# Layers 2 and 3 of a four-layer mixture kernel: activations of a bank's halves behind both halves' passes, and TensorE's order by a written plan of 359 steps

## The chip, the cores and the metric

One Trainium2 chip, one core of it. The metric is the device time of one launch in microseconds (us), the median of several runs. The core has TensorE (PE), VectorE (DVE), ScalarE (ACT), GpSimd (POOL) and SyncE (SP), each with its own instruction queue, worked off in order, and DMA engines that the queues hand transfers to. [...]

## The reference

The input x has 4 rows of 512 tokens with 256 features. Four layers follow one another, each of the form `x = x + ffn(cond(x))`. They are counted from 1 here. This case is about layers 2, 3 and the first row of layer 4:

```python
# layer 2: cond is one matrix per row; ffn is 15 experts, the best 3 of each token, and a shared expert
z   = x @ w_bot[b].T + bias
top_p, top_i = top_k(softmax(z @ router_W + router_b), 3)
routed = sum over the 3:  top_p * (relu(z @ eW1[e] + eb1[e]) @ eW2[e] + eb2[e])
x   = x + relu(z @ sW1 + sb1) @ sW2 + sb2 + routed
# layer 3: cond is W_base plus a low-rank part mixed by the row's cond; ffn is for half of the tokens
z   = x @ (W_base + 2 * sum_e w[e] Bs[e] As[e]).T + b_base
top_s, top_i = top_k(z @ w_router, 256)
up  = sigmoid(top_s) * (gelu(z[top_i] @ W1 + b1) @ W2 + b2)
x   = x + scatter_add(z, top_i, up)
# layer 4, cond: a shared gated MLP and the row's 2 best of 8 gated MLPs (hidden size 1024 each)
z   = mlp(x; shared) + sum over 2:  w * mlp(x; skill)      # mlp: (gelu(x Wg) * (x Wu)) Wd
```

All matrices are float32.

## The kernel before, in words

x of row b is kept transposed in SBUF, `x[b]` of 128 partitions by 2 by 512 tokens. A matmul's group of passes goes to one PSUM bank (`bank()`); most matmuls of all layers are recorded by one helper, `mm`, and so stand at line L102 of the profile, told apart by their tiles.

The kernel is written as Python generators: every part of the work yields between steps, and helpers interleave them. `weave(main, side, r)` takes r steps of `side` after each of `main`; `zipped` takes one of each in turn; `late(items, begin, end, lag)` begins an item and ends the one `lag` before it. Inside `tc.manual_schedule(engines={...})` the engines named keep the order in which the code issues; everywhere else a planner of the framework orders each engine's instructions by its own costs. The first layer is already written so: `in_turn(parts, FIRST_PLAN)` takes the generators' next steps in the order of a string, for TensorE alone. From layer 2 on, `other_layers()` (L1909 on) weaves the parts loosely, and the planner orders all engines until near the kernel's end.

The parts that matter, with the letters that the plan gives them:

- **E**, `l1_experts` (L1193): tokens are grouped by expert in 62 units of 128 tokens, worked in 38 blocks (24 pairs, 14 single units); the first 54 units hold all that row 0 needs. Each block has four stages: `fetched` (its expert's 512 KB of weights by SP; one indirect gather per unit by POOL, L1212, from the rows in `zd` into a tile `hs`), `turned` (transposes on TensorE, L1226, a copy on DVE, L1228), `hidden` (four matmuls into the two halves of one bank, and an ACT Relu with bias for each half, L1240, into a tile `bc` of which there are three), and `down` (matmuls that the profile writes as bank<-w,bc, a DVE copy, L1252, and a write to HBM, `yd<-bc`, L1253). The stages of a block lie 0, 2, 3 and 4 blocks behind.
- **Q**, `l1_places`, and **W**, `l2_weights`: small; index arithmetic on DVE, and layer 3's matrix per row.
- **S2, S3**, `l1_shared` of rows 2 and 3 (rows 0 and 1 were done before): the shared expert.
- **K0 to K3**, `l1_combine`: 12 indirect gathers per row from `yd` (POOL, L1302: 4 tiles of tokens, 3 experts each), scaled on ACT (L1311) and added on DVE (L1313), then 8 transposes (L1319) and an add to x (L1320).
- **D0 to D3**, `l2_cond`: matmuls x,p into z (ACT, L1367), the router's score (z,wr; ACT, L1374), z's rows written to HBM, a rank of the 512 scores on DVE (L1380 to L1418, ending in a tile `at`), a matmul s_token,at, then `who` on DVE, `x += z` on POOL (L1441), and two gathers of the chosen rows (POOL, L1444).
- **F0 to F3**, `l2_ffn`: transposes (L1457), four pairs of hidden passes with an ACT Gelu for each half of the bank (L1471), down passes, a bias add (DVE, L1484), the write `yd2` to HBM (L1486).
- **G0 to G3**, `l2_back`: four gathers (POOL, L1493), scaled on ACT (L1500), transposed (L1502), added to x (DVE, L1504).
- **X**, `l3_cond(0)`: row 0 of layer 4, 24 steps of four x,w and two a,w matmuls of 128x512 with a Gelu (L1545) and a product (L1551), its weights loaded by SP (`in_w3c`, 512 KB each).

Row 0 goes first: K0, D0, F0, G0 and X depend on each other in this order, and rows 1 to 3 follow beside. After X come `l3_prepare` (its first matmuls are bank<-w,pe) and rows 1 to 3 of layer 4 with the attention woven in.

In `hidden` of both E and F the code was, for each half of the bank, the passes and then its activation. The next half's passes go to the same bank, which the activation reads, and the framework makes them wait for it.

Of the kernel before, what the change touches and what calls it, by code (L numbers as in the profile page):

```python
# [21 lines left out]
KD = D // P  # L22
NT = S // P
FIRST_PLAN = """C0*3 L C0*10 H0 C1*2 H0*3 P C1*2 H0*3 C1*2 P H0 P C1*2 P H0 C1 L H0*2 P C1 H0 C1 H0*3 C1*2 P H0 H1 P C2 H1*4 P*2 C2*2 P H1*2 C2*2 H1 P*2 H1 P C2 H0 H1 P C2 H0 H1 C2 P C2 H1 H0 H1 C2 P H1*2 C2 P H1*2 C2*2 P*2 H1 T0*3 P T0 L H2 P*2 C3 H2*3 C3 H1 H2 P C3*3 P*2 H2 P H2 U0 C3*3 H2*2 P*2 H2 P*2 H2 C3 H2*2 P H2 C3 U0 H2 P*2 C3 H2*2 C3*2 H3*2 P U0 P U0*2 P H2 H3*2 U0*4 H3 U0 H3 U0*2 H3 U0 H3 U0*3 H2 H3 U0*4 H3*2 U0*4 H3 U0 J0 H3 U0 B U0*2 H3 U0 H3 U0*10 B*2 U0*3 B U0 H3 U0*3 H3*2 T1*3 U0 U1 U0 U1*3 T1 P U1 U0 U1*7 J0*3 U1*3 J0 U1*2 J0 U1*4 J0 A0 H3 U1 A0 U1*2 J0 U1 A0*3 U1 A0 U1*3 A0 U1 A0 J1 A0 U1*3 J1 U1*2 J1*3 U1 A0 J1*2 U1*2 A1 U1*2 A1 U1 A1*2 J2 U1*4 A1*2 U1*2 A1 U1 J2*2 L A1 O0 A1 O0 J2 U1 O0 A1 O0*7 J1 J2 O0 J2*2 O1 O0*3 J2 O0 A2 O0 O1 O0 A2 O1*3 R0 A2 R0 O1*2 A2 O1 A2*2 O1*4 J3 A2 O0 J3 O1 R0 A2 O1 J3 O1 A2 R0 J3 R0*2 J3 R0*6 J3 R0 A2 J3 O1*2 R0 O1 R0 A3 R0*4 J3 A3*2 R1*2 R0*2 A3 R1 R0 A3 R1*4 A3 R1 A3*2 R1*3 O2 R0 O2*2 R1*2 A3 R1 O2*2 A3 R1*2 O2 R1 O2*7 R1*2 O3 O2 R1*2 O3 O2*2 R1*2 O3 O2 O3*2 R2 O3*3 R2*2 O3 R2*3 O3 R2*2 O3 R2*5 R0 R2 O3*2 R1 O2 R2*2 O3*3 R2 O3 R3*2 R2*2 R3*2 O3 R3*2 R2 S0 R3 R2 R3 S0*3 R3 R2*2 R3*5 S1 R3*2 R2 S1 R3*7 V R3 V*3 S1*2"""

NEG = -1e30

# [26 lines left out]
def kernel(  # L54
# [1138 lines left out]
    def l1_experts():  # L1193

        pairs = [((g + 1) / EARLY, 2 * g, 2) for g in range(EARLY)]
        alone = [((i + 0.5) / SINGLES, 2 * EARLY + i, 1) for i in range(SINGLES)]
        blocks = [b[1:] for b in sorted(pairs + alone)] + [(j, 2) for j in range(FIRST, LIVE, 2)]
        rows = yd.rearrange("(u p) f -> u p f", p=P)
        held = {}

        def owner(j):
            return nc.values_load(
                table["of"][0:1, j : j + 1], engines=[mybir.EngineType.SP], min_val=0, max_val=14,
                skip_runtime_bounds_check_because="from the table, which holds no others",
            )

        def fetched(s):
            j, n = blocks[s]
            w = weight(ws[W_EXP + owner(j)])
            t = new(apool, [P, KD, S], "hs", bufs=4)  # L1210
            for u in range(n):
                nc.gpsimd.indirect_dma_start(  # L1212
                    out=t[:, 0, u * D : (u + 1) * D],
                    out_offset=None,
                    in_=zd[:, :],
                    in_offset=bass.IndirectOffsetOnAxis(ap=table["who"][:, j + u : j + u + 1], axis=0),
                )
            held[s] = w.rearrange("p (l k f) -> p l k f", l=2, k=KD), t

        def turned(s):  # L1220
            j, n = blocks[s]
            t = held[s][1]
            pt = bank().rearrange("p (k t) -> p k t", k=KD)
            for u in range(n):
                for k in range(KD):
                    nc.tensor.transpose(pt[:, k, tok(u)], t[:, 0, u * D + k * P :][:, :P], ident)  # L1226
            xT = t[:, 1].rearrange("p (k t) -> p k t", k=KD)
            nc.vector.tensor_copy(xT[:, :, : n * P], pt[:, :, : n * P])  # L1228

        def hidden(s):  # L1230
            j, n = blocks[s]
            w, t = held[s]
            xT = t[:, 1].rearrange("p (k t) -> p k t", k=KD)
            hy = new(apool, [P, 2, S], "bc", bufs=3)
            h = hy[:, 0].rearrange("p (m t) -> p m t", m=KD)
            ph = bank().rearrange("p (m t) -> p m t", m=KD)
            for m in range(KD):
                for k in range(KD):
                    mm(ph[:, m, : n * P], w[:, 0, k, tok(m)], xT[:, k, : n * P], k == 0, k == KD - 1)
                nc.scalar.activation(  # L1240
                    h[:, m, : n * P], ph[:, m, : n * P], AF.Relu, bias=table["bias"][:, m, j : j + 1]
                )
            held[s] = w, hy, h

        def down(s):
            j, n = blocks[s]
            w, hy, h = held.pop(s)
            py = bank()
            for u in range(n):
                for k in range(KD):  # L1250
                    mm(py[:, u * D : (u + 1) * D], h[:, k, tok(u)], w[:, 1, k], k == 0, k == KD - 1)
            nc.vector.tensor_copy(hy[:, 1, : n * D], py[:, : n * D])  # L1252
            nc.sync.dma_start(  # L1253
                out=rows[j : j + n].rearrange("u p f -> p u f"),
                in_=hy[:, 1, : n * D].rearrange("p (u f) -> p u f", f=D),
            )

        for s in range(len(blocks) + 4):
            for stage, lag in ((fetched, 0), (turned, 2), (hidden, 3), (down, 4)):
                if 0 <= s - lag < len(blocks):  # L1260
                    stage(s - lag)
            yield

    rows1 = {}

# [30 lines left out]
    def l1_combine(b):  # L1296
        got = []
        for r in range(3):
            got.append(new(wpool, [P, 1024], "w").rearrange("p (i f) -> p i f", i=NT))
        for i in range(NT):  # L1300
            for r in range(3):
                nc.gpsimd.indirect_dma_start(  # L1302
                    out=got[r][:, i],
                    out_offset=None,
                    in_=yd[: FIRST * P] if b == 0 else yd[:, :],
                    in_offset=bass.IndirectOffsetOnAxis(ap=rows1[b][:, r, i : i + 1], axis=0),
                )
        yield
        for i in range(NT):
            y = got[0][:, i]  # L1310
            nc.scalar.activation(y, y, AF.Copy, scale=gate1[b][:, 0, i : i + 1])  # L1311
            for r in range(1, 3):
                nc.vector.scalar_tensor_tensor(y, got[r][:, i], gate1[b][:, r, i : i + 1], y, ALU.mult, ALU.add)  # L1313
            if i % 2:
                yield
        for k in range(KD):
            pk = bank()
            for i in range(NT):
                nc.tensor.transpose(pk[:, tok(i)], got[0][:, i, tok(k)], ident)  # L1319
            nc.vector.tensor_add(x[b][:, k], x[b][:, k], pk)  # L1320
        yield


    z2, gate2, who2, back2, y2 = {}, {}, {}, {}, {}
# [36 lines left out]
    def l2_cond(b):  # L1361
        z = new(apool, [P, KD, S], "z", bufs=3)
        for m in range(KD):
# [1 line left out]
            for k in range(KD):  # L1365
                mm(pz, w2m[b // 2][:, b % 2, k, tok(m)], x[b][:, k], k == 0, k == KD - 1)
            nc.scalar.activation(z[:, m], pz, AF.Identity, bias=col("b_base", m))  # L1367
        yield

        psc = bank()  # L1370
        for k in range(KD):
            mm(psc, wr[:, k], z[:, k], k == 0, k == KD - 1)
        sc = new(apool, [P, S], "t", bufs=4)
        nc.scalar.copy(sc, psc)  # L1374
        zd2 = new(dram, [S, D], "zd2", bufs=2)
        run(rows_to_dram(z, zd2))
        sown = small([P, NT], "sown")
        unused = new(apool, [P, S], "pe", BF16)
        for i in range(NT):
# [71 lines left out]
    def l2_ffn(b):  # L1451
# [11 lines left out]
        def hidden(f2):  # L1463
            ph = bank().rearrange("p (f t) -> p f t", f=2)
            h = new(apool, [P, 2, D], "p4", bufs=4)
            for j in range(2):
                f = 2 * f2 + j
                wa = w2a[f // 4].rearrange("p (k f) -> p k f", k=KD)
                for k in range(KD):
                    mm(ph[:, j], wa[:, k, tok(f % 4)], xT[:, k], k == 0, k == KD - 1)  # L1470
                nc.scalar.activation(h[:, j], ph[:, j], AF.Gelu_apprx_tanh, bias=col("b1", f))  # L1471
            return h

# [16 lines left out]
    def l2_back(b):  # L1490
# [8 lines left out]
        for i in range(NT):  # L1499
            nc.scalar.activation(got[:, i], got[:, i], AF.Copy, scale=gate2[b][:, i : i + 1])  # L1500
            for k in range(KD):
                nc.tensor.transpose(pk[k][:, tok(i)], got[:, i, tok(k)], ident)  # L1502
        for k in range(KD):
            nc.vector.tensor_add(x[b][:, k], x[b][:, k], pk[k])  # L1504
        yield
# [403 lines left out]
    def other_layers():  # L1909
# [2 lines left out]
        gates3.clear()  # L1912
        w2c = weight(ws[W_L2])
        w2m[:] = [new(apool, [P, 2, KD, D], "p4", bufs=4) for _ in range(2)]
        weave(l1_experts(), chain((l1_places(b) for b in range(B)), l2_weights()), 0.3)
        wsh = weight(ws[W_EXP + 15])
        w2a[:] = [weight(ws[W_L2 + 1 + i]) for i in range(2)]
        w2b[:] = [weight(ws[W_L2 + 3 + i]) for i in range(2)]
        combine = [l1_combine(b) for b in range(B)]
        next(combine[0])  # L1920
        run(l1_shared(2, wsh))
        run(combine[0])
        cond2 = l2_cond(0)
        next(cond2)
        next(combine[1])
        weave(cond2, l1_shared(3, wsh))
        shared.clear()
        ahead3[0, 0] = l3_expert_weights(0, 0)

        others = zipped(*(  # L1930
            chain(range(8 * (b - 1)), combine[b], l2_cond(b), l2_ffn(b), l2_back(b)) for b in range(1, B)
        ))
        weave(chain(l2_ffn(0), l2_back(0)), others, 0.8, rest=False)
        weave(l3_cond(0), others, 1.4)
        w3qo = weight(ws[W_QO])
        w3m = new(wpool, [P, 1024], "w")
        nc.sync.dma_start(out=w3m[:, :656], in_=l3m)
# [167 lines left out]
```

## Time and profile before

| what | us |
|---|---|
| three runs | 1490.92, 1487.20, 1482.77 |
| their median | 1487.2 |
| the profiled execution | 1487.06 |
| its span (first to last instruction) | 1485.3 |
| first matmul of E's blocks in this stretch to the start of the stage after X | 458.6 to 905.6 |
| X's first matmul | 700.02 |
| mean granted clock of TensorE | 0.937 |

The profile is of one execution. Busy time is given for each engine, and for a group of instructions (line, engine, operation, `out<-in` by tile names, shape, count) the busy time, the mean of one in ns, and the idle time of the engine just before them with what ended it. The granted clock is TensorE's, 1.00 at full speed. A table by stretches gives for each window its length and the busy time (and count) of PE, PE's weight loads, DVE, ACT and POOL, then the granted clock, the busy share of the DMA engines and GB/s.

### The profile page before, as it was taken

To read this page: it belongs to the slowest core of one execution; us is meant where nothing else is said; L and a number is where in the kernel's file an instruction comes from. 1 tells how busy PE (TensorE), PEld (TensorE's weight loads), DVE (VectorE), ACT (ScalarE), POOL (GpSimd) and SP (SyncE) were. 2 spreads that over 40 slices of the span, in tenths; PEclk is the share of its full clock that TensorE was granted. 3 is DMA by queue.
4 is the path that set the end of the run, shared out by engine and by line. 5 is a ranking of instruction groups with operands and counts; after the bars stand their busy time and mean duration, and the time that the engine had idled before them with its cause. 6 is when DMAs were issued, how large, how long until landed. Compare 5 with 4: busy or idle time off the path is not lost.

```text
span 1485.3 us, 13849 instructions
## 1 busy us (share of the span) xinstructions
PE 1305.3 (88%) x4342; PEld 717.1 (48%) x4342; DVE 727.6 (49%) x1661; ACT 348.2 (23%) x599; POOL 511.6 (34%) x387
## 2 busy tenths in 40 slices
PE   6998656787979898657999899999999999999988
PEld 3546544444446787324545544444444444444443
DVE  2766213247585233333143113893589259826952
ACT  3443112122011222123232112222222322241010
POOL 0044455330204434632221110541064005447961
PEclk9999869897988999878999999999999999999999
DMA  6424756732207886531132210021202112111102
GB/s 248 122 75 138 179 158 163 176 90 88 57 15 240 292 292 202 158 128 57 50 107 82 96 52 1 0 71 43 86 0 71 52 63 70 57 57 43 57 15 73
DMA packets 96897, 149.36 MB, mean 101 GB/s; under 512 B 26943, under 2 KB 66382, under 8 KB 96814
## 3 DMA queue, kind: packets, MB, share of 16 engines
q1 hardware_dynamic: 85870, 119.53, 24.5%
q0 software_dynamic: 10944, 28.85, 7.8%
q8 instruction: 37, 0.61, 0.2%
q14 instruction: 46, 0.38, 0.1%
HBM read 124.48 MB, written 23.86 MB: 100 GB/s over the span
## 4 chain that ended last, share of the span: by engine, by line
PE 68%; DVE 8%; DMA 8%; issue 8%; POOL 3%; ACT 2%; SPq 1%; another core or an unknown queue 0%; POOLq 0%; DVEq 0%; ACTq 0%
PE bank L102 65%; DMA yd<-bc 3%; DMA w<-in_ws_dram 1%; DMA hs<-zd,who 1%; POOL p L1670 1%; PE bank L722 1%; DVE r_u L543 1%; DMA yd<-t 1%; PE bank L586 1%; DVE r_t L545 1%; DVE pe L1393 1%; POOL bc L1493 1%; PE bank L1226 0%; DMA w<-yd,rows 0%; SPq L702 0%
## 5 line engine op out<-in xcount | busy, mean ns | idle before, releaser
L102 PE MATMUL bank<-x,w 128*128 128x512 f32 x896 | 417.8, 609 | 4.8 <-DMA w<-in_w0c_dram 4.8
L102 PE MATMUL bank<-a,w 128*128 128x512 f32 x576 | 281.1, 616 | 6.1 <-POOL a L806 4.4
L102 PEld LDWEIGHTS bank<-x,w 128*128 128x128 f32 x896 | 170.3, 195 | 209.6 <-issue 200.6
L102 PE MATMUL bank<-hs,w 128*128 128x256 f32 (+2 forms) x624 | 194.6, 445 | 20.7 <-ACT bc L1240 11.4
L1670 POOL TENSOR_TENSOR p<-pe,vv 128x1024 f32<-128x1024 f32 x42 | 119.1, 2870 | 222.1 <-DVE pe L1663 222.1
L102 PEld LDWEIGHTS bank<-a,w 128*128 128x128 f32 x576 | 110.6, 197 | 134.9 <-issue 126.0
L102 PEld LDWEIGHTS bank<-hs,w 128*128 128x128 f32 x624 | 110.0, 195 | 94.8 <-issue 56.2
L1545 ACT ACTIVATE t<-bank 128x512 f32<-128x512 f32 x96 | 57.3, 597 | 250.0 <-PE bank L102 249.7
L1551 DVE SCALAR_TENSOR_TENSOR a<-bank,w,t 128x512 f32<-128x512 f32 x64 | 47.8, 747 | 113.5 <-PE bank L102 107.6
L1212 POOL DMA_INDIRECT hs<-zd,who x62 | 59.0, 951 | 122.4 <-PE bank L102 50.0
L1679 DVE TENSOR_REDUCE pe<-p 128x64 f32<-128x1024 f32 x64 | 77.1, 1215 | 23.8 <-POOL p L1670 23.7
L710 POOL DMA_INDIRECT hs<-zd,who x62 | 59.3, 956 | 77.3 <-issue 33.4
L102 PE MATMUL bank<-w,hs 128*128 128x192 f32 x248 | 60.3, 392 | 25.6 <-DMA w<-in_ws_dram 22.1
L1651 DVE TENSOR_REDUCE bank<-p 128x64 f32<-128x1024 f32 x64 | 78.2, 1221 | 0.9
L102 PE MATMUL bank<-w,bc 128*128 128x256 f32 x248 | 64.9, 387 | 0.0
L102 PEld LDWEIGHTS bank<-w,hs 128*128 128x128 f32 x248 | 50.0, 233 | 30.5 <-issue 21.6
L1302 POOL DMA_INDIRECT w<-yd,rows x48 | 45.4, 946 | 51.0 <-PE bank L102 22.0
L1240 ACT ACTIVATE bc<-bank,eb_of 128x256 f32<-128x256 f32 (+1 forms) x76 | 33.0, 434 | 124.7 <-PE bank L102 81.9
L102 PE MATMUL bank<-w,w 128*128 128x512 f32 (+1 forms) x176 | 59.7, 479 | 0.0
L1640 DVE TENSOR_TENSOR p<-bank,vv 128x1024 f32<-128x1024 f32 x48 | 58.4, 1218 | 0.5
L1548 DVE TENSOR_TENSOR a<-bank,t 128x512 f32<-128x512 f32 x32 | 22.0, 688 | 68.6 <-PE bank L102 55.4
L806 POOL TENSOR_TENSOR a<-at,bc 128x512 f32<-128x512 f32 x16 | 20.3, 1269 | 97.7 <-PE bank L102 45.8
(443 smaller groups left out, 1633.2 us busy)
## 6 DMA issues: line engine op xcount, KB each, us to landing
w<-in_ws_dram SPq DMA_DIRECT2D x62, 512.0 KB
w<-in_w3c_dram SPq DMA_DIRECT2D x48, 512.0 KB
bc<-gd SPq DMA_DIRECT2D x32, 256.0 KB
w<-in_ws_dram SPq DMA_DIRECT2D x62, 128.0 KB
bc<-gd SPq DMA_DIRECT2D x15, 512.0 KB
w<-in_w0c_dram SPq DMA_DIRECT2D x12, 512.0 KB
zd<-h SPq DMA_DIRECT2D x12, 512.0 KB
yd<-bc SPq DMA_DIRECT2D x24, 256.0 KB
```

Of the source, the lines that this page charges most:

```text
L102: nc.tensor.matmul(o, lhsT, rhs, start=start, stop=stop)
L710: nc.gpsimd.indirect_dma_start(out=t[:, 0, u * D : (u + 1) * D], out_offset=None, in_=zd0[g][:, :], in_offset=bass.IndirectOffsetOnAxis(ap ...
L1212: nc.gpsimd.indirect_dma_start(out=t[:, 0, u * D : (u + 1) * D], out_offset=None, in_=zd[:, :], in_offset=bass.IndirectOffsetOnAxis(ap=tab ...
L1240: nc.scalar.activation(h[:, m, : n * P], ph[:, m, : n * P], AF.Relu, bias=table["bias"][:, m, j : j + 1])
L1302: nc.gpsimd.indirect_dma_start(out=got[r][:, i], out_offset=None, in_=yd[: FIRST * P] if b == 0 else yd[:, :], in_offset=bass.IndirectOffs ...
L1545: nc.scalar.activation(gl, pg, AF.Gelu_apprx_tanh)
L1548: nc.vector.tensor_tensor(h, pu, gl, ALU.mult)
L1551: nc.vector.scalar_tensor_tensor(h, pu, share, gl, ALU.mult, ALU.mult)
L1640: engine.tensor_tensor(pq, q[:, c * QH : (c + 1) * QH, None, :].to_broadcast([P, QH, 16, 16]), kv[:, None, :, 0, :].to_broadcast([P, QH, 1 ...
L1651: nc.vector.tensor_reduce(raw[:, hs], pq, AX.X, ALU.add)
L1670: (nc.vector if near else nc.gpsimd).tensor_tensor(pv, (raw if near else at)[:, hs, None, :].to_broadcast([P, QH, 16, 16]), kv[:, :, 1, :] ...
L1679: nc.vector.tensor_reduce(of[:, c * QH : (c + 1) * QH], pv, AX.X, ALU.add)
```

## The change

TensorE's order from E to X is written down: a second string, SECOND_PLAN, of 359 steps, and `other_layers()` hands the parts to `in_turn` inside a manual schedule for TensorE. So that the plan can cut finely, E yields after each stage of a block (152 steps instead of 42), and `l1_combine`, `l2_cond` and `l2_back` yield more often. DVE, ACT, POOL and SP stay with the planner, which orders them anew around the code's new order. In `hidden` of E and F both halves' passes now come first, then both activations. Instruction kinds and counts are the same; FIRST_PLAN and the order after X are untouched. In the plan X's last steps stand before F3's last passes and most of G2 and G3.

```diff
+SECOND_PLAN = """E*4 W E*4 Q E*3 Q*2 E Q E*7 W E*3 Q E*2 W E*2 W E*24 W E*8 W E*60 L E*24 L E*3 K0 E*2 K0 E K0 S2 K0*2 S2 E*2 K0*5 D0*2 E K0 D0 E K1*4 D0*2 S2 D0 S3 D0 S2 S3 D0*3 L K1 S3 D0 K1*2 F0 K1*2 S3 K1*2 F0 K2 F0*2 D1 F0*2 D0 K2 K3*2 K2 K3 D1 F0 K2*2 G0 D1 D0 F0 G0 D1*2 K2 D1 G0 D1 G0*2 D1*2 K2 G0*2 D1 K2*3 K3 D1 X*2 G0 K2 K3 K2 X*2 K3 F1 X*2 F1 D2 D1 K3 X*2 D2 X F1 D2 X F1 K3 X F1 D2 F1 X K3 F1 D2*2 K3 X K3 D3 G1 X*2 D2*2 K3 G1 X D2 D3 X D2 X D3 G1 D2*2 F1 D3 F2 G1 D3 X F2 X D3 F2 D3*2 G1*2 F2*2 X D3 F2 G1 X F2 X*2 G1 F3 G2 D3 F2 X D3 G2 F3*2 X D3 F3*3 G2 F3 G3*3 G2*4 G3*5 G2 F3"""
...
 def hidden(s):                                     # E; the same edit in F's hidden
             for m in range(KD):
                 for k in range(KD):
                     mm(ph[:, m, : n * P], w[:, 0, k, tok(m)], xT[:, k, : n * P], k == 0, k == KD - 1)
+            for m in range(KD):
                 nc.scalar.activation(
                     h[:, m, : n * P], ph[:, m, : n * P], AF.Relu, bias=table["bias"][:, m, j : j + 1]
                 )
...
             for stage, lag in ((fetched, 0), (turned, 2), (hidden, 3), (down, 4)):
                 if 0 <= s - lag < len(blocks):
                     stage(s - lag)
-            yield
+                    yield
...
-        weave(l1_experts(), chain((l1_places(b) for b in range(B)), l2_weights()), 0.3)
-        wsh = weight(ws[W_EXP + 15])
-        w2a[:] = [weight(ws[W_L2 + 1 + i]) for i in range(2)]
-        w2b[:] = [weight(ws[W_L2 + 3 + i]) for i in range(2)]
-        combine = [l1_combine(b) for b in range(B)]
-        next(combine[0])
-        run(l1_shared(2, wsh))
-        run(combine[0])
-        cond2 = l2_cond(0)
-        next(cond2)
-        next(combine[1])
-        weave(cond2, l1_shared(3, wsh))
         shared.clear()
-        ahead3[0, 0] = l3_expert_weights(0, 0)
-
-        others = zipped(*(
-            chain(range(8 * (b - 1)), combine[b], l2_cond(b), l2_ffn(b), l2_back(b)) for b in range(1, B)
-        ))
-        weave(chain(l2_ffn(0), l2_back(0)), others, 0.8, rest=False)
-        weave(l3_cond(0), others, 1.4)
...
+        parts = {"L": loads(), "E": l1_experts(), "Q": places(), "W": l2_weights()}
+        parts.update({f"S{b}": second_layer(b) for b in range(2, B)})
+        for b in range(B):
+            parts.update({f"K{b}": l1_combine(b), f"D{b}": l2_cond(b), f"F{b}": l2_ffn(b), f"G{b}": l2_back(b)})
+        parts["X"] = l3_cond(0)
+        with tc.manual_schedule(engines={mybir.EngineType.PE}):
+            in_turn(parts, SECOND_PLAN)
```

L is `loads()`: the shared expert's weights, layer 3's four weight tiles, and the first weights of X, issued at three steps of the plan.

More of the change, by code (lines that the diff above doesn't have):

```diff
@@ L1307, in l1_combine @@
                 )
-        yield
+            yield
         for i in range(NT):
@@ L1313, in l1_combine @@
                 nc.vector.scalar_tensor_tensor(y, got[r][:, i], gate1[b][:, r, i : i + 1], y, ALU.mult, ALU.add)
-            if i % 2:
-                yield
+            yield
         for k in range(KD):
@@ L1320, in l1_combine @@
             nc.vector.tensor_add(x[b][:, k], x[b][:, k], pk)
-        yield
+            yield
     z2, gate2, who2, back2, y2 = {}, {}, {}, {}, {}
@@ L1367, in l2_cond @@
             nc.scalar.activation(z[:, m], pz, AF.Identity, bias=col("b_base", m))
-        yield
+            yield
         psc = bank()
@@ L1374, in l2_cond @@
         nc.scalar.copy(sc, psc)
+        yield
         zd2 = new(dram, [S, D], "zd2", bufs=2)
-        run(rows_to_dram(z, zd2))
+        yield from rows_to_dram(z, zd2)
         sown = small([P, NT], "sown")
@@ L1470, in hidden @@
                     mm(ph[:, j], wa[:, k, tok(f % 4)], xT[:, k], k == 0, k == KD - 1)
+            for j in range(2):
+                f = 2 * f2 + j
                 nc.scalar.activation(h[:, j], ph[:, j], AF.Gelu_apprx_tanh, bias=col("b1", f))
@@ L1502, in l2_back @@
                 nc.tensor.transpose(pk[k][:, tok(i)], got[:, i, tok(k)], ident)
+            yield
         for k in range(KD):
@@ L1914, in other_layers, with loads, places, second_layer @@
         w2m[:] = [new(apool, [P, 2, KD, D], "p4", bufs=4) for _ in range(2)]
-        weave(l1_experts(), chain((l1_places(b) for b in range(B)), l2_weights()), 0.3)
-        wsh = weight(ws[W_EXP + 15])
-        w2a[:] = [weight(ws[W_L2 + 1 + i]) for i in range(2)]
-        w2b[:] = [weight(ws[W_L2 + 3 + i]) for i in range(2)]
-        combine = [l1_combine(b) for b in range(B)]
-        next(combine[0])
-        run(l1_shared(2, wsh))
-        run(combine[0])
-        cond2 = l2_cond(0)
-        next(cond2)
-        next(combine[1])
-        weave(cond2, l1_shared(3, wsh))
-        shared.clear()
-        ahead3[0, 0] = l3_expert_weights(0, 0)
-        others = zipped(*(
-            chain(range(8 * (b - 1)), combine[b], l2_cond(b), l2_ffn(b), l2_back(b)) for b in range(1, B)
-        ))
-        weave(chain(l2_ffn(0), l2_back(0)), others, 0.8, rest=False)
-        weave(l3_cond(0), others, 1.4)
+        shared.clear()
+        wsh = []
+        def loads():
+            wsh.append(weight(ws[W_EXP + 15]))
+            yield
+            w2a[:] = [weight(ws[W_L2 + 1 + i]) for i in range(2)]
+            w2b[:] = [weight(ws[W_L2 + 3 + i]) for i in range(2)]
+            yield
+            ahead3[0, 0] = l3_expert_weights(0, 0)
+            yield
+        def places():
+            for b in range(B):
+                l1_places(b)
+                yield
+        def second_layer(b):
+            yield from l1_shared(b, wsh[0])
+        parts = {"L": loads(), "E": l1_experts(), "Q": places(), "W": l2_weights()}
+        parts.update({f"S{b}": second_layer(b) for b in range(2, B)})
+        for b in range(B):
+            parts.update({f"K{b}": l1_combine(b), f"D{b}": l2_cond(b), f"F{b}": l2_ffn(b), f"G{b}": l2_back(b)})
+        parts["X"] = l3_cond(0)
+        with tc.manual_schedule(engines={mybir.EngineType.PE}):
+            in_turn(parts, SECOND_PLAN)
         w3qo = weight(ws[W_QO])
```

## The prediction, made before the changed kernel ran

> **What bounds the kernel now.** I read the page first (busy shares, slices), then stretches of time, the groups and waits of the stretch that the change touches (458.6 to 905.6 us), and the timeline around its long gaps.
>
> ```profile
> span 1485.3 us, 13849 instructions
> PE 1305.3 (88%) x4342; PEld 717.1 (48%) x4342; DVE 727.6 (49%) x1661; ACT 348.2 (23%) x599; POOL 511.6 (34%) x387
> PE   6998656787979898657999899999999999999988
> ```
>
> TensorE (PE) is busy 88%; from slice 21 on it is all but full, and from 905.6 us on nothing else limits, so what the region saves or loses arrives 1:1 at the end. The region's losses lie in slices 13 to 20 (a slice is 37.1 us). By stretches (window, length, PE busy, ..., granted clock, DMA share, GB/s):
>
> ```profile
> 500.00:520.00 20.00, 17.51 (x96) 14.61 (x96) 5.96 (x11) 4.57 (x11) 7.62 (x9) 1.00 0.90 299
> 598.00:609.00 11.00, 6.07 (x16) 4.88 (x17) 3.68 (x8) 2.25 (x5) 6.63 (x7) 0.69 0.40 119
> 645.00:656.00 11.00, 1.11 (x6) 0.68 (x6) 8.34 (x41) 4.92 (x7) 0.27 (x1) 0.69 0.46 144
> 686.00:700.00 14.00, 3.97 (x21) 2.07 (x20) 8.56 (x43) 6.37 (x10) 4.26 (x4) 0.64 0.34 95
> 875.00:905.60 30.60, 30.60 (x69) 13.24 (x68) 4.74 (x7) 3.66 (x7) 0.00 (x0) 0.95 0.00 0
> ```
>
> Three states: an experts' stage (to 598) with short waits and a DMA share of 0.90; a middle (598 to 700) with long gaps and a low clock; row 0's layer 4 (from 700.02), nearly full. What ends PE's waits, first for the stage to 598, then 458.6 to 700 (us, times, longest):
>
> ```profile
> L102 PE MATMUL bank<-hs,w 128*128 128x256 f32 (+2 forms) x301 | 67.5, 347 | 11.9 <-ACT bc L1240 11.4 <-DVE hs L1228 0.4
> L1240 ACT ACTIVATE bc<-bank,eb_of 128x256 f32<-128x256 f32 (+1 forms) x74 | 32.0, 433 | 124.7 <-PE bank L102 81.9 <-DMA yd<-bc 21.6 <-DVE hs L1228 11.4
> ```
>
> ```profile
> PE bank L102 <- DVE at L1418: 12.3, 2, 9.9
> PE bank L102 <- ACT bc L1240: 11.4, 11, 2.6
> PE bank L102 <- issue: 10.7, 3, 5.3
> PE bank L1502 <- ACT bc L1500: 7.4, 3, 5.8
> PE bank L102 <- ACT w L1311: 5.3, 1, 5.3
> ```
>
> The second half's passes wait for ACT on the first half of their bank; ACT itself had waited 21.6 us, 8 times, for the write yd<-bc to free one of three bc buffers. The gaps of the middle are the chain of row 0: gathers, sort (at), second gathers.
>
> **The change, part by part.** PE work from the experts' start, by cadences in the trace, is the same in both: experts 134.5 us, layer-2 weights 3.9, two shared parts 18, combines 3.5, four conds (D0 to D3) 25, four ffns (F) 57, four backs (G) 3.5, X (row 0's layer 4) 24 x 5.16 = 124; sum 369.6. The region takes 447.0, so some 63 us are idle, 12 are slow clock, 2 joints. Only these 77 can move.
>
> *Halves.* Both halves' passes now stand ahead of both activations, in E (experts) and F. Removed: the 13.0 us of PE waits in E (14 waits, 11.4 by the row plus small ones). Added: ACT starts the first half 0.87 us (two 128x256 matmuls at 0.433) later, which is hidden, as the block's down pass follows a stage later, 4 to 5 us behind. The late thing next is that down pass: an activation that waits for yd<-bc now holds PE at its first w,bc matmul, with about 2 us more slack. Bounds: 0 to 13 us stay. DMA at 0.90 can give at most a tenth more rate, and the pieces of yd<-bc in the chain of waits last 5 to 7 us; I take 4 left, so 9 gained, and block 33 (the last that row 0 needs) ends at 579 instead of 587.9. Call that end e.
>
> Here a rule can be weighed. The granted clock is 1.00 in each of seven stretches from 458.6 to 598, in spite of 14 waits of about a microsecond. The Trainium skill, TensorE: Matmul & The Clock Gate, section "A second HAM failure mode: psum-queue depth-cycling", says that small idles between groups, repeated, make the clock swing between half and full. By it removal would gain more than idle time: were a fifth of 130 us at half speed, some 13 us more (an estimate). The rows show none, so I add 0. Where gaps exceed 5 us the trace does show half speed: eight x,p matmuls took 5.57 us at 624.80 after 5.3 idle, against 3.60 at full clock; I charge 2 us for each such gap.
>
> *Middle, from e.* Before, the planner ordered PE; now SECOND_PLAN does, the other engines' queues being planned around it. By dependencies and 1.25 us per indirect gather (0.95 busy + 0.30 between, L1302): K0's 12 gathers run e+4 to e+18 and its last DVE step ends e+21. TensorE fills the span with the remaining blocks and shared parts and idles 6 (before: 5.3). D0's x,p and z,wr end e+31, block 37 goes in at e+32.5, its yd lands e+38, so K1's gathers start e+38 and end e+53 (36 gathers of K1 to K3 = 45 us of POOL). New queueing:
> - DVE: row 0's sort (at, L1418) stands behind two combine steps L1313; its matmuls wait to e+46 (PE idle 3). The who of row 0 stands behind an L1313 that waits for K1's ninth gather: e+51.
> - POOL: row 0's two z2 gathers (L1444) stand behind K1's twelve and three of K2: e+57. F0's transposes come at e+61; PE idles 8 to 9. Before, POOL was free there and the gather came 1.1 us after the sort's result (656.40).
> - ACT: F0's first gelus stand behind L1311 of K2 and K3; the third pair's waits for K3's tile gathered at e+82: PE idle 6 at e+79 to e+85.
> - SP: F0's yd2 write stands behind four 512 KB loads (w3c), +3.
>
> F0's last down ends e+90; write, four gathers (L1493), scale, transposes and the x add, which in DVE stands behind D1's sort, put X's first matmul at e+107 to e+113: 686 to 692, I take 690 against 700.02. In short, the 9.9, 5.8 and 5.3 us gaps of before give way to 6, 3, 8.5 and 6; the gain of E survives and little is added.
>
> *X's stretch.* After 700 PE idles 13.6 us before, as eight waits for L1500, two for hs gathers and gelus. The plan packs F1 to F3 and D1 to D3 between X's steps; each of their gathers is issued some steps ahead. I leave 3 idle plus 2 slow; 167.4 us of work: X's last matmul at 690 + 172 = 862.
>
> *Tail.* Before, row 3's chain ran under X:
>
> ```profile
> 857.57 1.89 PE L102 MATMUL bank<-w,p 128*128 128x256 f32 x8
> 860.28 0.39 SPq L1486 DMA_DIRECT2D yd<-t  x1
> 866.85 1.01 POOL L1493 DMA_INDIRECT bc<-yd,back  x1 [22.83 <-DMA yd<-t]
> 870.00 0.51 ACT L1500 ACTIVATE bc<-bc,gate 128x256 f32<-128x256 f32 x1 [3.04 <-DMA bc<-yd,back]
> 874.43 0.69 PE L1502 MATMUL bank<-ident,bc 128*128 128x128 f32 x2 [0.94 <-ACT bc L1500]
> 874.91 3.31 PE L102 MATMUL bank<-x,w 128*128 128x512 f32 x4
> ```
>
> From F3's last down (859.3) to the last transposes (874.9) is 15.6 us, with X's matmuls between; X then ran on to 905.6. In the plan 14.2 us of F3 and the whole of G3 stand after X's last step, so the chain is bare: 862 + 14.2 + 15 + 2 slow = 893, the start of the next stage, against 905.62.
> The write's share of it is where the second rule bears. The trace has yd<-t at 5.82 us beside w3c loads and 3.0 in a quiet stretch (808.86). The Trainium skill, DMA: Bandwidth & Descriptors, section "Anatomy of one DMA — SWDGE (gpsimd) path", gives 2.0 us plus bytes over 436 GB/s, 2.6 us for 256 KB (an estimate; that path is GpSimd's, this write is SP's). By the row the bare chain is 15, by the rule 12. Row 1's loads are near, so I take 15.
>
> Sum: E 587.9 to 579, -9; from there to X 112.1 becomes 111, -1; from X's first matmul to the next stage 205.6 becomes 172 + 14.2 + 17 = 203, -2.5: together -12.5, about 893 for 905.6. The profiled execution took 1487.06 us (span 1485.3), the median of three is 1487.2; so the sum gives 1474.6; I round the clock's part up and give 1476. Three runs spread by 8 us, so about 0.5% (7.4 us) is what can be told from no change.
>
> **Rivals.** *(a) Larger gain.* E's waits vanish wholly (579 becomes 575) and the z2 gathers and gelus, whose positions I worked out by hand, wait less than 8.5 and 6. For: of the 139.4 us to 598 PE is busy 125.9, and waits for nothing else. Against: DMA at 0.90. Saves 10 to 20 more: 1456 to 1466.
> *(b) Given back.* The half-wait only becomes a wait of D on the same buffers, that is, the change doesn't do there what it says, with PE idle as before; e stays at 586. For: ACT's wait for yd<-bc (21.6) is not touched by the order of two activations, and bc stays at three. The rest gives -3: 1481 to 1492.
> *(c) Slower.* POOL's in-order queue. Row 0's two gathers stand behind fifteen others, themselves behind block 37's write. In before K1's first gather took 4.64 us to land (613.20), against 2.8 in general, and the region's write pieces reach 7.4. Each us by which block 37's write is late moves K1, who, z2, F0 and X by the same. If it and the gathers come 20 us later than worked out, X starts at 710; the bare tail (15) stays: 913, so 1494 to 1508. It decides from 12 us of lateness on (from 20 by more than 0.5%); PE has no other work by then, as the plan's order fixes what comes next.
>
> **How the numbers follow.** Forecast 0.40 (1467 to 1483); (a) 0.20; (b) 0.20; (c) 0.20. Faster by over 0.5% (below 1479.8): 0.36 of the forecast and all of (a), 0.56; same: 0.04 + 0.18 = 0.22; slower (above 1494.6): 0.20 of (c) and 0.02 of (b), 0.22. For 8 in 10 the range leaves out half of (a)'s and half of (c)'s: 1459 to 1501. The forecast's own range is 1467 to 1483.
>
> **What would show it.** In the profile after: no waits of hs,w matmuls for L1240, and instead waits of w,bc ones; K0's first gather at 580 to 584 (591.8 before); F0's transposes (L1457 before) about 8 us after PE's last work, behind POOL's L1302; a gelu (L1471) behind L1311; X's first x,w at 686 to 692; after X's last step one gap of 12 to 15 us ahead of the last transposes (L1502); the next stage's w,pe near 893. K0's gathers at 590 or later would make (b) right, X beyond 705 would make (c) right, and a full X stretch with a tail under 8 us would make me too careful.

## The result

The changed kernel takes 1476.44 us (median of 20 runs, 1469.07 to 1488.84) against 1490.36 us before (20 runs, 1482.77 to 1497.62): ratio 0.9909, 95% interval 0.9888 to 0.9929. It is faster, by some 14 us. The profiled execution took 1476.93 us (span 1475.2).

The page after, its span, busy line and TensorE's slices:

```profile
span 1475.2 us, 13843 instructions
PE 1311.4 (89%) x4342; PEld 729.8 (49%) x4342; DVE 728.4 (49%) x1661; ACT 342.7 (23%) x599; POOL 514.6 (35%) x387
PE   6998757796979998828999979999999999999988
```

The slices of the experts' stage are full now, one slice (the 18th) has fallen to 2, and X's are nines from the 20th to the 23rd; in the 24th X ends. The stretches that answer to those shown of before (window, length, PE, weight loads, DVE, ACT, POOL, clock, DMA share, GB/s):

```profile
500.00:520.00 20.00, 19.81 (x109) 17.26 (x108) 6.23 (x12) 4.61 (x12) 8.83 (x10) 1.00 1.00 345
640.00:660.00 20.00, 2.19 (x7) 1.46 (x6) 3.35 (x7) 0.86 (x1) 12.44 (x13) 0.59 0.39 118
680.00:691.80 11.80, 5.61 (x28) 5.04 (x29) 9.63 (x46) 5.90 (x10) 5.15 (x5) 0.59 0.24 61
860.00:886.40 26.40, 16.47 (x76) 13.41 (x74) 2.78 (x6) 5.60 (x13) 3.80 (x4) 0.82 0.35 110
```

In the experts' stage TensorE is busy 19.8 of 20 us where it was 17.5, and the DMA engines are at 1.00 where they were at 0.90. In return there are 20 us at 640 in which TensorE does almost nothing, and a gap at the end of X. By marks in the two profiles (us; E's first transposes, the 458.6 of the table ahead of the prediction, come 1.3 us before its first hs,w passes):

| stretch | before | after | difference |
|---|---|---|---|
| start to E's first hs,w matmul | 459.9 | 456.5 | -3.4 |
| from there to K0's first gather | 131.9 | 117.0 | -14.9 |
| K0's first gather to X's first matmul | 108.3 | 118.4 | +10.1 |
| X's first matmul to the next stage (w,pe) | 205.6 | 194.6 | -11.0 |
| the rest, TensorE's order unchanged | 579.7 | 588.8 | +9.1 |
| span | 1485.3 | 1475.2 | -10.1 |

What TensorE waited for in E (groups of the stretch 456.4 to 580: busy, mean ns | idle before it) and, below, its waits from 458 to 700:

```profile
L103 PE MATMUL bank<-hs,w 128*128 128x256 f32 (+1 forms) x296 | 58.4, 340 | 0.2 <-issue 0.2
L103 PE MATMUL bank<-w,bc 128*128 128x256 f32 x227 | 55.0, 380 | 0.0
...
L1242 ACT ACTIVATE bc<-bank,eb_of 128x256 f32<-128x256 f32 (+1 forms) x74 | 28.1, 430 | 89.2 <-PE bank L103 44.7 <-DMA yd<-bc 34.0 <-issue 9.1
```

```profile
PE bank L103 <- ACT p L1475: 20.0, 1, 20.0
PE bank L1506 <- ACT bc L1504: 6.6, 2, 5.1
PE bank L1459 <- DMA hs<-zd,who: 4.6, 2, 3.7
PE bank L103 <- DVE w L1315: 3.8, 1, 3.8
PE bank L1320 <- issue: 3.4, 1, 3.4
PE bank L1320 <- DVE w L1315: 3.3, 1, 3.3
```

ACT waits for the writes yd<-bc even more than before (34.0 us against 21.6), but TensorE no longer waits for ACT here: both hs,w and w,bc passes stand at 0.2 us or less. The second list is led by one wait of 20.0 us of row 0's first w,p passes for a gelu.

### The profile page after: what moved, and what is told of

Read it like the earlier page. It is cut to its first block, busy times and chain, and to the rows that moved or that the text cites. A ratio compares the mean times of both kernels' runs of the same rounds, so it can differ in the third digit from the quotient of the medians.

```text
span 1475.2 us, 13843 instructions
## 1 busy us (share of the span) xinstructions
PE 1311.4 (89%) x4342; PEld 729.8 (49%) x4342; DVE 728.4 (49%) x1661; ACT 342.7 (23%) x599; POOL 514.6 (35%) x387
## 4 chain that ended last, share of the span: by engine, by line
PE 60%; POOL 5%; issue 4%; DVE 4%; DMA 2%; another core or an unknown queue 1%; ACT 1%; POOLq 0%; DVEq 0%
PE bank L103 58%; POOL hs L1213 2%; POOL p L1675 1%; DMA w<-yd,rows 1%; POOL w L1304 1%; DMA bc<-yd,back 1%; DVE pe L1684 0%; PE bank L1227 0%; DMA hs<-zd,who 0%; POOL hs L1769 0%; POOL bc L1497 0%; POOL w L1769 0%; DMA yd<-bc 0%; PE bank L1320 0%
## 5 line engine op out<-in xcount | busy, mean ns | idle before, releaser
L103 PE MATMUL bank<-hs,w 128*128 128x256 f32 (+2 forms) x624 | 186.8, 446 | 2.1 <-issue 2.1
L103 PEld LDWEIGHTS bank<-hs,w 128*128 128x128 f32 x624 | 113.2, 199 | 66.6 <-issue 56.7
L103 PE MATMUL bank<-w,hs 128*128 128x192 f32 x248 | 63.7, 409 | 16.2 <-DMA w<-in_ws_dram 12.5
L103 PE MATMUL bank<-w,bc 128*128 128x256 f32 x248 | 59.9, 380 | 0.0
L1304 POOL DMA_INDIRECT w<-yd,rows x48 | 46.4, 967 | 26.8 <-issue 13.4
L1254 DVE COPY bc<-bank 128x512 f32<-128x512 f32 (+1 forms) x38 | 22.5, 592 | 62.0 <-PE bank L103 35.7
```

Source lines behind the costliest of these rows:

```text
L103: nc.tensor.matmul(o, lhsT, rhs, start=start, stop=stop)
L1304: nc.gpsimd.indirect_dma_start(out=got[r][:, i], out_offset=None, in_=yd[: FIRST * P] if b == 0 else yd[:, :], in_offset=bass.IndirectOffs ...
```

## The experiments

Eleven runs in three groups, each group on a chip of its own (the quoted expectations say "call" for a group). The kernel before ran in each group and took 1489.7, 1473.9 and 1468.4 us, so only ratios to it, or runs of one group, are compared. Which chip the two kernels of the result ran on is not on record. The first group took the change apart.

**The halves alone.** The kernel before, and in both `hidden`:

```diff
                     mm(ph[:, m, : n * P], w[:, 0, k, tok(m)], ...)
+            for m in range(KD):
                 nc.scalar.activation(
```

> The kernel before with one edit of the change: in E's and F's hidden both halves' passes stand ahead of both activations; the order stays the planner's. Theory A (the 13 us of TensorE waits in E come from the order of the halves): the waits of hs,w matmuls for L1240 vanish, at most 3 us of them come back at the down passes, E ends 9 to 13 us earlier, and the middle and X are as before: 1477 to 1481 us, ratio to before 0.991 to 0.994. Theory B (the cause is the bc buffers held by the yd<-bc writes, which the edit leaves alone): the waits move to the down passes nearly whole: 1487 to 1491 us, ratio 0.998 to 1.001.

Measured: 1477.03 us, ratio 0.9909 (0.9879 to 0.9938), the same as the whole change. K0's first gather comes 119.0 us after E's first hs,w matmul (131.9 before), the stretch from there to X is 108.4 (108.3), X 209.7 (205.6). The groups of E:

```profile
L102 PE MATMUL bank<-hs,w 128*128 128x256 f32 (+2 forms) x308 | 63.7, 350 | 0.4 <-DVE some L1977 0.4
L102 PE MATMUL bank<-w,bc 128*128 128x256 f32 x248 | 62.0, 389 | 6.3 <-ACT w L1312 3.7 <-ACT bc L1241 2.6
...
L1241 ACT ACTIVATE bc<-bank,eb_of 128x256 f32<-128x256 f32 (+1 forms) x76 | 29.0, 432 | 112.3 <-PE bank L102 65.1 <-DMA yd<-bc 40.0 <-issue 7.1
```

Theory A holds, theory B falls. ACT's wait for the writes is longer than ever (40.0 us, 15 times), and only 2.6 us of it reach TensorE, at the down passes. In the kernel before, 8 of TensorE's 11 waits for L1240, and 10.2 of their 11.4 us, stand behind an activation that had itself waited for yd<-bc. So the writes were the reason why ACT was late, and the order of the halves was the reason why TensorE felt it.

**The plan alone.** The changed kernel with that edit undone.

> The changed kernel with the activations put back behind each half's passes: the plan alone. Theory A: some 10 to 13 us of waits for L1240 return in E, while the middle and the tail are those of the changed kernel: 1486 to 1490 us, level with before (0.997 to 1.001). Theory B: E runs as in the changed kernel, because it is the plan's order of E's stages that keeps bc free: 1475 to 1479 us (0.990 to 0.993).

Measured: 1527.04 us, ratio 1.0236 (1.0199 to 1.0273): slower than before by 37 us, outside both expectations. TensorE's first waits, 456 to 700 us:

```profile
PE bank L103 <- ACT bc L1241: 34.6, 37, 6.4
PE bank L103 <- DVE at L1419: 3.4, 1, 3.4
```

37 waits for 38 blocks, at least 0.51 us each: in the written order the second half's passes always stand straight behind the first's, so TensorE waits for a whole activation in almost every block. In 13 of them the activation had waited for yd<-bc (14.5 us), and the last wait, behind K0's first gather, took 6.4. The planner of the kernel before had put other passes between the halves where it could, so that it waited only 11 times. E takes 155.1 us here, 23 more than before, and the stretch from K0 to X 126.8, 18.5 more. With the written order the halves' edit is not a part of the gain but what makes the order bearable.

**The end of the plan.** The changed kernel; in SECOND_PLAN the last steps become

```diff
-... G1 X F2 X*2 G1 F3 G2 D3 F2 X D3 G2 F3*2 X D3 F3*3 G2 F3 G3*3 G2*4 G3*5 G2 F3
+... G1 X F2 G1 F3 G2 D3 F2 D3 F3*6 G3 X*2 G2*5 X*3 G3*6
```

> The changed kernel with the end of the plan reordered: F3's passes come ahead of X's last five steps, two of these follow G3's gathers, then G2's transposes, then three, then G3's. Theory A (the bare chain write, gathers, scale, transposes behind F3 costs its full length, and the clock after it): the gap of 9 us ahead of the last transposes goes, and the 3.5 us of slow clock behind it: the next stage starts at about 875 instead of 886.4, and the kernel takes 1463 to 1467 us, 0.991 to 0.993 of the changed kernel. Rival: F3, now earlier, waits for its own gathers or G2 for F2's write, and the gap only moves: within 4 us of the changed kernel.

Measured: 1454.58 us, ratio 0.9762 (0.9728 to 0.9796), in the first group, where the changed kernel didn't run. This is the end of X in the changed kernel's profile:

```profile
869.35 3.62 PE L103 MATMUL bank<-w,p 128*128 128x256 f32 x16
...
873.78 0.38 SPq L1490 DMA_DIRECT2D yd<-t  x1
878.34 0.95 POOL L1497 DMA_INDIRECT bc<-yd,back  x1 [30.32 <-DMA yd<-t]
...
882.25 0.69 PE L1506 MATMUL bank<-ident,bc 128*128 128x128 f32 x2 [9.07 <-ACT bc L1504]
...
885.77 0.69 PE L1506 MATMUL bank<-ident,bc 128*128 128x128 f32 x2 [0.57 <-ACT bc L1504]
...
886.38 2.07 PE L103 MATMUL bank<-w,pe 64*128 64x512 f32 x2
888.39 6.40 PE L103 MATMUL bank<-x,w 128*128 128x512 f32 x8
```

The reordered end once more, beside the changed kernel, on the third chip:

> The changed kernel with F3 ahead of X's last five steps, now beside the changed kernel itself. From the profiles, the next stage starts 8 to 9 us earlier and its first matmuls save 3.5 us of slow clock: 10 to 13 us below the changed kernel, 0.991 to 0.993 of it. In the first call it came out 21 us below by the ratios; if that is the edit's own and not the scatter of runs, it comes out so again.

1429.29 us, 0.9753 (0.9718 to 0.9788) of before, and 0.9893 of the changed kernel's 1444.72 us in that group: 15 us below, for 10 to 13 expected. The profile of this run at the end of X:

```profile
820.28 1.89 PE L103 MATMUL bank<-hs,w 128*128 128x256 f32 x8
822.01 3.62 PE L103 MATMUL bank<-w,p 128*128 128x256 f32 x16
825.46 3.60 PE L103 MATMUL bank<-x,w 128*128 128x512 f32 x8
828.90 1.88 PE L103 MATMUL bank<-a,w 128*128 128x512 f32 x4
...
840.07 1.04 PE L1506 MATMUL bank<-ident,bc 128*128 128x128 f32 x8
841.04 1.12 PE L103 MATMUL bank<-w,pe 64*128 64x512 f32 x2
```

No line has an idle time in brackets, and w,pe takes 1.12 us instead of 2.07: the chain from F3's last w,p to G3's transposes lies under five steps of X, and the next stage starts at full clock. From X's first matmul to w,pe it takes 183.4 us against 194.3 in the changed kernel of the same group, 10.9 less, which is what was expected of the edit. The medians differ by 15 and the two profiled executions by 25; the rest lies in stretches that the edit doesn't touch (6.6 us ahead of E, 7.8 behind w,pe).

**ACT and POOL in the plan's order.** The changed kernel with `manual_schedule(engines={PE, Activation, Pool})`.

> The changed kernel with ACT and POOL also held to the plan's order between E and X. Theory A (row 0's 20 us wait ahead of F0's first down pass comes from the order of ACT and POOL: gelus behind the scaling of K2 and K3, the two z2 gathers behind three of K2): both go, F0's first down pass follows its gelus within 3 us, X starts 15 to 20 us earlier, 1458 to 1466 us (0.988 to 0.993 of the changed kernel). Rival (the signals from TensorE themselves arrive late while POOL issues gathers back to back, as the two adds of K1 at 644 and 655 us suggest): the gap stays at 10 us or more, within 5 us of the changed kernel. Third: the plan's order is bad for POOL or ACT elsewhere in E: slower.

Measured: 1468.87 us, ratio 0.9853 (0.9819 to 0.9888); X starts at 682.80 instead of 691.81. The stretch from K0 to X takes 109.0 us instead of 118.4. That is half of what theory A asked: two waits are left in ACT that no recorded instruction ends, of 9.7 and 7.6 us. The rival had named such waits, but its "within 5 us" did not come either: by the ratios the run is some 8 us below the changed kernel.

**Signals that come late.** In the profile of the changed kernel, these are the steps around the 20 us gap (628 to 664, all engines; "remote" is a wait whose end the trace can't put down to an instruction):

```profile
631.93 1.91 PE L1320 MATMUL bank<-ident,w 128*128 128x128 f32 x8
...
644.13 0.69 DVE L1321 TENSOR_TENSOR x<-x,bank 128x512 f32<-128x512 f32 x1 [8.40 <-remote]
...
654.62 0.33 SPq L107 DMA_DIRECT2D w<-in_w3c_dram  x1
654.63 0.69 DVE L1321 TENSOR_TENSOR x<-x,bank 128x512 f32<-128x512 f32 x1 [9.81 <-remote]
...
661.71 1.57 ACT L1475 ACTIVATE p<-bank,pc 128x256 f32<-128x256 f32 x4 [20.85 <-remote]
...
662.24 2.07 PE L103 MATMUL bank<-w,p 128*128 128x256 f32 x4 [20.04 <-ACT p L1475]
```

K1's eight transposes are recorded at 631.93 to 633.8. The two adds of DVE wait only for the first and the second four of them, yet start at 644.13 and 654.63; SP's load, which waits for the same second four, is issued at 654.62; ACT's gelus wait for passes recorded at 635.8 to 642.2 and start at 661.71. So three engines get TensorE's signals 11 to 22 us late, if its matmuls ended when the profile says, while POOL issues gathers back to back, from 607.96 to 656.1. In the kernel before there is such a hole of 5.0 us at 642.1 to 647.1, behind POOL's gathers up to 642.9. To break that run of gathers I kept ACT and POOL in the plan's order and moved K2's gathers behind G0's and K3's into X:

```diff
-F0 K2 F0*2 D1 F0*2 D0 K2 K3*2 K2 K3 D1 F0 K2*2 G0 D1 D0 F0 G0 D1*2 K2 ... X*2 G0 K2 K3 K2 X*2 K3 F1 ...
+F0 F0*2 D1 F0*2 D0 D1 F0 G0 D1 D0 F0 K2*4 G0 D1*2 ... X*2 G0 K3*4 X*2 K2*4 F1 X*2 F1 K2*4 X D2 ...
```

> As the run with ACT and POOL in the plan's order, but the gathers of K2 stand behind G0's four, and those of K3 behind the first two steps of X, so that POOL's longest run of gathers without a pause is K1's twelve and row 0's two instead of 38. Theory A (signals from TensorE reach ACT and DVE late while POOL issues gathers back to back): the waits of ACT in F0 that no recorded instruction ends (9.7 and 7.6 us in the run before this one) fall below 3 us in sum, X starts at 660 to 668 instead of 682.8 us, 1450 to 1458 us, 0.987 to 0.993 of that run. Rival (the waits belong to F0 itself, its table load or its gelus): X starts within 4 us of 682.8, no gain. Third: K2 and K3, now late, hold up D2 and D3, and TensorE idles in X's stretch: X starts early, but the end is level.

Measured: 1433.99 us, 0.9753 (0.9705 to 0.9801) of before in its group. The longest run of gathers behind K0's is 16, the stretch from K0 to X takes 93.1 us, and no such wait is left. But the run doesn't show that the shorter runs of gathers are the reason, because another run of the same group, on the same chip, has none either:

> The changed kernel with the halves' edit undone in F alone (E keeps it). In the run with both undone, the waits for gelus were thirteen of 0.56 us and the long one; so 7 to 9 us slower than the changed kernel if these waits are TensorE's own time: 1483 to 1486 us. Rival (the planner of ACT moves with it and the long wait changes): outside that by over 5 us either way.

Measured: 1458.05 us, ratio 0.9895 (0.9858 to 0.9932). Here POOL issues 38 gathers in a row from 593 to 641, and no wait of ACT or DVE is without a recorded end. Against the changed kernel of the next group (0.9842) it is some 8 us slower by the ratios, as expected of F's half of the edit, but across two groups; the intervals overlap, so it is not shown. Four kernels were then run beside the one before on a third chip:

> The changed kernel once more, beside three others on one chip: in the last call TensorE's signals were never late (no wait in ACT or DVE without a recorded end, though POOL issued 38 gathers in a row), and the kernel before took 1473.9 us there against 1489.7 in the call ahead of it. Theory A' (the late signals depend on the chip or the moment, and on a long run of gathers): where they are missing, the 20 us wait ahead of F0's first down pass shrinks to what order alone makes of it, some 4 to 8 us, and the change gains more, 0.978 to 0.985 of before; where they are there, it is 16 to 21 us again and 0.989 to 0.993. Rival (the wait is the order's own): 20 us in either case.

> The kernel before with the halves' edit alone, on the same chip as the changed kernel. If late signals are missing on this chip, the plan should show a gain of its own here: this run 8 to 14 us above the changed kernel; if they are there, level with it within 5 us, as in the first call (both 0.991 of before).

> ACT and POOL in the plan's order, K2's and K3's gathers behind G0's, on the same chip as the changed kernel. With late signals on this chip: their waits in 620 to 680 us fall from 17 to 21 us (changed kernel) to below 3, and the kernel is 20 to 26 us below the changed one. Without them: the order alone gains, X starts 10 to 14 us earlier, 12 to 18 us below the changed kernel.

Measured in this group: the changed kernel 1444.72 us, 0.9842 (0.9809 to 0.9876); the halves alone 1458.77, 0.9923 (0.9893 to 0.9953); the spread gathers 1432.84, 0.9771 (0.9739 to 0.9803). None has a late signal. The same steps of the changed kernel:

```profile
618.08 1.91 PE L1320 MATMUL bank<-ident,w 128*128 128x128 f32 x8
...
621.75 1.28 DVE L1321 TENSOR_TENSOR x<-x,bank 128x512 f32<-128x512 f32 x2
...
626.93 0.84 ACT L1475 ACTIVATE p<-bank,pc 128x256 f32<-128x256 f32 x2
...
642.11 0.51 ACT L1313 ACTIVATE w<-w,gate 128x256 f32<-128x256 f32 x1 [3.95 <-DMA w<-yd,rows]
642.53 0.82 ACT L1475 ACTIVATE p<-bank,pc 128x256 f32<-128x256 f32 x2
643.03 6.00 PE L103 MATMUL bank<-w,p 128*128 128x256 f32 x16 [6.19 <-ACT p L1475]
```

The adds follow at once, and what is left of the gap is 6.19 us: the third pair's gelus stand in ACT behind an L1313 that waits for a gather of K3. So of the 20 us, 6 are the order's, and the other 14 come with the late signals. All six profiles of before, the changed kernel and the first group have such waits, and the seven of the other two groups, on two other chips, have none. Nor are they confined to this stretch. The changed kernel's list of them:

```profile
ACT p L1475 <- remote: 20.8, 1, 20.8
DVE x L1321 <- remote: 18.2, 2, 9.8
ACT hs L724 <- remote: 12.4, 2, 6.6
DVE a L734 <- remote: 6.5, 2, 4.8
ACT h L588 <- remote: 3.7, 1, 3.7
```

The last three lines lie at 199 to 333 us, ahead of E, in code that the change leaves alone; the other five profiles have such waits there too, of up to 12.3 us. E's first hs,w matmul comes at 455.2 to 461.9 us in these six profiles and at 435.8 to 445.2 us in the seven without. TensorE may not be the only sender: the changed kernel's trace holds 836, 1370 and 444 updates of the main semaphores of TensorE, VectorE and ScalarE, for 893, 1529 and 503 instructions that make one. The trace of the same kernel on the third chip holds 893, 1528 and 504. So updates were merged there, or their records lost.

That the waits come with the chip or the moment, for the same kernel, is what these runs show. A long run of gathers is not enough to make them: three profiles without them have 38 in a row. What makes them stays open, and so does whether a long run is needed: the kernels with short runs never met a chip that had late signals.

The spread gathers are 12 us below the changed kernel here, at the near end of the 12 to 18 expected. The stretch from K0 to X takes 91.5 us instead of 103.8, but X's takes 201.0 instead of 194.3: ten more matmuls now lie in it (4.2 us), and 2.5 us more are idle. To that extent the third theory, that late K2 and K3 hold up X's stretch, holds.

Where late signals are missing, the plan has a gain of its own: 1458.77 to 1444.72, 14 us. With them it had none by the ratios (0.9909 for the halves alone in the first group, 0.9909 for both in the result). By stretches of the profiles, plan and halves against halves alone: E -2 with late signals and +2 without, X -14 to -15 in either case, and the stretch from K0 to X -2 without late signals, +10 with them.

**Both orders together.**

> The same with the reordered end of the plan (F3 ahead of X's last five steps). Theory A: the two gains lie in different stretches and add up: 11 to 15 us below the run without it, 1437 to 1446 us, the fastest of all. Rival: X, earlier, comes to its end before F3's gathers are in, and TensorE waits there: less than 5 us gained.

Measured: 1431.23 us, 0.9704 (0.9665 to 0.9743) of before: the lowest ratio of all, but less than 3 us below the run without the reordered end, so the size that the rival gave. Its reason, TensorE waiting at X's end, is not what the profile shows: X's stretch is 9.1 us shorter (192.0 against 201.1) and idle 5.7 us instead of 12.4, much as in the other pair, while the time up to E was 6 us longer and the time behind w,pe 3 us longer. Its interval and that of the reordered end alone (0.9718 to 0.9788) overlap: which of the two is faster is not settled. Both beat the kernel before and the changed one.

## Why the prediction came out right, and which of its steps did not

The total was right (1476 forecast, 1476.4 measured), and E and X's stretch moved the way forecast. The terms were not of the right size, the stretch from K0 to X moved the other way, and the rest moved though it was taken as fixed. That the errors cancelled so closely is luck. (The parts of the prediction's sum give 369.4, not 369.6; nothing hangs on it.)

- *Halves in E* (forecast -9, 4 of 13 us staying). Measured -14.9 from E's first hs,w to K0's first gather. Of 13.0 us of waits 1.3 are left, 1.1 of them for gathers. The step that failed is the 4 us taken as left, from "DMA at 0.90 can give at most a tenth more rate": the share did rise by a tenth, to 1.00, with 15% more rate (299 to 345 GB/s), and TensorE did not wait for a write. The slack at the down pass was enough for the waits for the writes, in the written order, and nearly so in the planner's. The other 3 us are busy time: up to block 33's down pass TensorE is busy 113.1 us where it was 116.3, for the same matmuls at the same granted clock. Why is not shown.
- *The clock in E.* It stayed at 1.00, so the reading of the clock by the rows held. The Trainium skill, TensorE: Matmul & The Clock Gate, section "A second HAM failure mode: psum-queue depth-cycling", reports the swing for a bf16 kernel with 512 columns; 14 waits of up to 2.6 us did not bring it about here.
- *From K0's first gather to X* (forecast -1, counted from block 33's end, 3.9 us earlier). Measured +10.1. The order's stalls were near the forecast: K0 6.7 for 6, the sort's matmuls 3.8 for 3, row 0's z2 gathers 4.6 for 8 to 9, behind K1's twelve and three of K2 as written, G0 5.1 + 1.5. The gelus were put at 6 and measured 20.0 here, and 6.2 where no signal was late. What the sum lacked is the 14 us of late signals. The profile before shows their like only as a 5 us hole here and three of 4.0 to 5.2 us ahead of E, and the forecast gave them no place.
- *X's start* was forecast at 690 and came at 691.8: E's surplus, a start of E 3.4 us earlier and the late signals cancelled, again by luck.
- *X's stretch* (forecast 5 us lost): no wait at all up to the tail, at a granted clock of 1.00. The stretch is 11.0 us shorter with the tail in it: 3.7 less idle (13.6 to 9.9) and 7.3 less busy, nine of its matmuls having moved elsewhere.
- *Tail* (forecast 15 + 2). From F3's last w,p (872.97) to w,pe (886.38) it took 13.4, 9.9 of it idle; the write took 3.8 us in the chain of waits, between the two rows of before (3.0 and 5.8), and 1.2 more than the 2.6 estimated by the Trainium skill, DMA: Bandwidth & Descriptors, section "Anatomy of one DMA — SWDGE (gpsimd) path", which is about GpSimd's path. The 13.4 lie about halfway between the 15 by the row and the 12 by the rule, so neither was the better guide. The slow clock cost some 3.7, not 2. The forecast saw the bare chain, and the reordered end shows what hiding it is worth: 10.9 us of X's stretch.
- *The rest* was taken as carrying 1:1. It lost 9.1: some 3.7 directly behind the tail's gap, 5.4 later. The idle time is the same, 14.0 us in both; the same 1447 matmuls are busy 574.8 us instead of 565.7, at a mean granted clock of 0.97 instead of 0.99. Over all thirteen profiles this stretch, always in the same order, takes 578.1 to 588.8 us, and the changed kernel alone 585.8 and 588.8; one profile each can't tell the later 5.4 from the scatter of executions.
- *Rival (b)*, that the edit would not do what it says, was wrong. *Rival (c)* had its place right (row 0's chain in the middle, POOL's gathers at work at the time) and named another mechanism: K1's gathers and block 37's write were on time.
- What the forecast did not ask is which half of the change earns the gain. On the first chip the halves alone had all of it by the ratios, and the plan without them was 37 us slower than before; on the third, without late signals, the halves alone gained 10 us and the plan 14 more.

## What to carry to other kernels

Where two evacuations read the two halves of one PSUM bank, put both halves' passes first: TensorE then meets a late evacuation only one stage later, and with the halves alone 40.0 us of waiting in ACT cost it 2.6. A hand-written order takes away what a planner slipped in between, so look for every place where the code relied on it (37 waits of half a microsecond and more here), and for the chain that stands bare at the plan's end: five steps of other work moved behind F3 were worth as much as the whole plan. Compare a stretch of a profile over several executions, and over chips, before explaining it: the +14 us of late signals, one of the largest terms here, came and went with the chip, and another +5 us can't be told from scatter.

## What was not expected of the hardware

- TensorE's signals reached DVE, SP and ACT 11 to 22 us late in one stretch. Such waits stand in all six profiles of the result and the first chip, and in none of the seven of two other chips. The kernel before took 1489.7 us on the first chip and 1468.4 and 1473.9 on the two others.
- The DMA engines ran at a share of 1.00 and 345 GB/s through 500 to 520 us of E, and in all of E TensorE met no wait of more than 0.6 us.
- A gap of 9 us ahead of the next stage cost some 3.7 us in slow matmuls behind it: eight x,w matmuls took 6.40 us (888.39) and w,pe 2.07, where the kernel before, without a gap there, took 3.70 and 1.12.
